# Two-layer attention on one core: scaling q and k after their product, and the second unit's norm moved into blocks 0 and 1

## The chip, the cores and the metric

The kernel runs on one core of a Trainium2 chip. The metric is the device time of one execution in microseconds (us). The engines named below are TensorE (PE, and PEld for its weight loads), VectorE (DVE), ScalarE (ACT), GpSimd (POOL) and SyncE (SP). They run beside each other, each through its own list of instructions in program order, and wait for one another by semaphores.

## What is computed

Sixteen images of 256 channels by 32 x 32 positions go through two layers. Each layer normalises the image over 16 groups, applies a four-headed attention with a position term, and adds the result to the image:

```python
def _L0_conv_ref(x, Wq, bq, Wk, bk, Wv, bv, rel_h, rel_w):
    xf = x.reshape(b, c, n)              # 16, 256, 1024
    def proj(Wt, bt):
        y = jnp.einsum('oc,bcn->bon', Wt, xf) + bt[None, :, None]
        return y.reshape(b, heads, d, n) # 4 heads of 64
    q, k, v = proj(Wq, bq), proj(Wk, bk), proj(Wv, bv)
    sim = jnp.einsum('bhdi,bhdj->bhij', q, k)
    rel = (rel_h + rel_w).reshape(heads, d, n)
    qpos = jnp.einsum('hdi,bhdj->bhij', rel, q)
    attn = jax.nn.softmax(sim + qpos, axis=-1)
    return jnp.einsum('bhdn,bhmn->bhdm', v, attn).reshape(b, c, w, h)

def _gn(v, G=16, eps=1e-5):              # the last axis is split into 16 groups of 2
    g = v.reshape(B_, H_, W_, G, C_ // G)
    m = jnp.mean(g, axis=(1, 2, 4), keepdims=True)
    s = jnp.var(g, axis=(1, 2, 4), keepdims=True)
    return ((g - m) / jnp.sqrt(s + eps)).reshape(v.shape)

x = x + _L0_conv_ref(_gn(x), ...)
x = x + _L1_conv_ref(_gn(x), ...)
```

A group is thus two of the 32 columns of an image, over all channels and rows.

## The kernel before

**Units and blocks.** A unit is one image in one layer; there are 32, in an order (`units`) that lets an image's second layer begin some units after its first. A unit has four blocks, b = 0 to 3: two pairs of heads (`pr`) by two halves of the 1024 positions (`half`). The loop at the end of `fast_path` calls `block(n)` 128 times. A block makes eight tiles of scores (j = 0 to 7): DVE writes the position term into PSUM (`seed`), PE adds the products of k and q onto it (`scores`), ACT takes the exponential to SBUF with a fixed shift in place of the row's maximum. DVE adds up the eight tiles for the denominators, with POOL's accumulating DMAs for the last one. PE multiplies them with v (`attend`), in two stretches of 3.45 us each, and ACT takes the product out of PSUM (`take_out`).

**Stretches.** `stretches` splits a set of products in two halves. The second half waits for a one-element memset on POOL, the token, which in turn waits for the first half; `word()` puts that memset into POOL's list.

**Work for coming units.** Within the blocks stand pieces for later units: `prepare` makes v, q, k and the position products of the next pair or the next unit. The norm of unit u+2 is made in unit u in three steps: `norm_sums` (ACT, one instruction per group with an accumulator that is read out after it, line 190), `norm_mean` (PE multiplies the sums with a constant matrix into the tile pm, line 209, and DVE takes the mean out), `norm_squares` (ACT, line 190 with the bias neg) and `norm_var` (PE line 209 again, DVE, then a power of minus one half and a product on POOL, lines 237 and 239). The scaled image xn of unit u+1 is made in unit u by `norm_apply` (ACT, one instruction per group, line 248). These pieces are cut into ranges of groups and placed by hand at four points of a block: after the first scores, before the second piece, before the first attend stretch, and after the seeds of the next block. In block 1 the third point reads:

```python
if b == 1 and two:
    norm_sums(u + 2, range(12, G))
if b == 1 and one:
    norm_apply(u + 1, range(9, 11))
...
po = psum2(ring[3], f"po_{n}")
values_of_p = attend(blk, po)
values_of_p(0)
if two and half == 1:
    if b == 1:
        mean_out = norm_mean(u + 2, filled(f1, f"pm_{n}", 0.0))
```

On PE the order there is: first attend stretch, the small products of `norm_mean`, the next block's first scores, second attend stretch.

**The beginning.** Unit 0 and unit 1 have nobody to make their norm. So DVE reduces image 0 (`reduced`), PE makes the mean, DVE centres the image (`centred`), ACT squares ten groups and DVE the other six, PE makes the variance and POOL the power (rstd0, line 886). ACT and DVE then scale xn of unit 0 in place (lines 910 and 913), and only then PE multiplies it into q and k. Meanwhile image 1 gets its reductions, mean and squares in the same way. The weights are loaded as they lie and transposed on PE (`transposed`), and ACT copies them out of PSUM (`taken`), in three sets raw0 (first layer's Wq and Wk), raw1 (both Wv) and raw2 (second layer's Wq and Wk).

PSUM has four tiles of two banks with the tags a to d; `ring` says which tag serves which purpose in a block, and changes places within the blocks.

Of the kernel before, what the change touches and what calls it, by code (L numbers as in the profile page):

```python
# [9 lines left out]
F32 = mybir.dt.float32  # L10
# [7 lines left out]
P = 128  # L18
# [34 lines left out]
def fast_path(ctx, tc, sh, x, layers, out, W, den_all, token, good, flag):  # L53
# [140 lines left out]
    def norm_sums(u, gs):  # L194
        if u not in reds:
            reds[u] = small.tile([P, G], F32, tag="red", name=f"red_{u}")
        for g in gs:
            of_group(u, g, AF.Identity, reds[u])
# [27 lines left out]
    def norm_squares(u, gs):  # L226
        for g in gs:
            of_group(u, g, AF.Square, sums[u], bias=negs[u][:, g : g + 1])
# [16 lines left out]
    def norm_apply(u, gs):  # L245
        rstd, shift = rss[u]
        for g in gs:
            nc.scalar.activation(  # L248
                grouped(xns[u], g),
                grouped(xt[units[u][0]], g),  # L250
                AF.Identity,
                bias=shift[:, g : g + 1],
                scale=rstd[:, g : g + 1],
            )
# [333 lines left out]
    ring = ["b", "c", "a", "d"]  # L588
# [29 lines left out]

    def block(n):
# [27 lines left out]
        for j in range(1, 4):  # L647
            scores(blk, j)
        (first, first_out), (second, second_out) = prepare(u, b)
        first(0)  # L650
        if b == 0 and one:
            norm_apply(u + 1, range(0, 1))
        if b == 1 and two:
            norm_sums(u + 2, range(9, 11))
# [3 lines left out]
        if b == 0 and one:  # L658
            norm_apply(u + 1, range(1, 5))
        if b == 1 and two:  # L660
            norm_sums(u + 2, range(11, 12))
        if b == 2 and two:
            norm_squares(u + 2, range(0, 5))
# [19 lines left out]
        add_up(blk, 2)  # L683
        if half == 0:
            second(1)
            second_out()
# [15 lines left out]
        if b == 0 and one:  # L702
            norm_apply(u + 1, range(5, 9))
        if b == 0 and two:
            norm_sums(u + 2, range(0, 2))
        if b == 1 and two:
            norm_sums(u + 2, range(12, G))
        if b == 1 and one:
            norm_apply(u + 1, range(9, 11))
        if b == 2 and two:  # L710
            norm_squares(u + 2, range(5, 11))
        po = psum2(ring[3], f"po_{n}")
        values_of_p = attend(blk, po)
        values_of_p(0)
        if two and half == 1:
            if b == 1:
                mean_out = norm_mean(u + 2, filled(f1, f"pm_{n}", 0.0))
            else:
                mean_out = norm_var(u + 2, filled(f1, f"pm_{n}", EPS / 2))
# [16 lines left out]
        if two and half == 1:  # L736
            mean_out()
# [3 lines left out]
        if b == 0 and two:  # L741
            norm_sums(u + 2, range(2, 9))
        if b == 1 and one:
            norm_apply(u + 1, range(11, G))
        if b == 2 and two:
            norm_squares(u + 2, range(11, G))
# [87 lines left out]
    def by_group(t, g0=0, g1=G):  # L834
        return t.rearrange("p c (w g t) -> p (c w) g t", g=G, t=GT)[:, :, g0:g1, :]

    def spread(t, g0=0, g1=G):
        return (
            t[:, g0:g1].unsqueeze(1).unsqueeze(3).to_broadcast([P, CC * sh.W, g1 - g0, GT])
        )  # L840

    def reduced(u, cc):
        nc.vector.tensor_reduce(
            reds[u][:, cc, :],
            xt[units[u][0]][:, cc, :].rearrange("p (w g t) -> p g w t", g=G, t=GT),
            AX.XY,
            ALU.add,
        )

    def first_mean(u, pm):  # L850
        red = reds.pop(u)
        for cc in range(CC):
            nc.tensor.matmul(pm, W.avg, red[:, cc, :], start=(cc == 0), stop=(cc == CC - 1))
        negs[u] = small.tile([P, G], F32, tag="neg", name=f"neg_{u}")
        nc.scalar.mul(negs[u], pm, -1.0)
        sums[u] = small.tile([P, G], F32, tag="sum", name=f"sum_{u}")
        xns[u] = gnpool.tile([P, CC, N], F32, tag="gn", name=f"xn_{u}")

    def centred(u, g0, g1):
        nc.vector.tensor_tensor(  # L860
            by_group(xns[u], g0, g1),
            by_group(xt[units[u][0]], g0, g1),
            spread(negs[u], g0, g1),
            ALU.add,
        )

    def rest_of_squares(u, g0):

        sq = ppool.tile([P, 2, HALF], F32, tag="p", name=f"first_sq_{u}")
        sq = sq.rearrange("p a n -> p (a n)")[:, : CC * sh.W * (G - g0) * GT].rearrange(  # L870
            "p (w g t) -> p w g t", g=G - g0, t=GT
        )
        nc.vector.tensor_tensor(sq, by_group(xns[u], g0), by_group(xns[u], g0), ALU.mult)
        nc.vector.tensor_reduce(
            sums[u][:, g0:], sq.rearrange("p w g t -> p g w t"), AX.XY, ALU.add
        )

    def first_var(u, pm):
        nc.tensor.matmul(pm, W.avg, sums.pop(u), start=True, stop=True)
        var = small.tile([P, G], F32, tag="var", name=f"var_{u}")  # L880
        nc.vector.tensor_scalar(var, pm, EPS, None, ALU.add)
        return var

    def first_rstd(u, var):
        rstd = small.tile([P, G], F32, tag="rstd", name=f"rstd_{u}")
        nc.gpsimd.tensor_tensor(rstd, var, W.mhalf[:, :G], ALU.pow)
        return rstd

    for u in range(2):
        reds[u] = small.tile([P, CC, G], F32, tag="first_red", name=f"first_red_{u}")  # L890
    G1, G2 = G // 2 + 2, G // 4
    pm0 = psum2("c", "pm_0")
    for cc in range(CC):
        reduced(0, cc)
    first_mean(0, pm0[:, 0, :G])
    transposed("a", *raw0)
    norm_squares(0, range(G1))
    centred(0, 0, G)
    rest_of_squares(0, G1)
    rstd0 = first_rstd(0, first_var(0, pm0[:, 1, :G]))  # L900
    taken(raw0[1])
    transposed("b", *raw1)
    taken(raw1[1])
    pm1 = psum2("d", "pm_1")
    for cc in range(CC):
        reduced(1, cc)
    first_mean(1, pm1[:, 0, :G])
    transposed("a", *raw2)
    for g in range(G2):
        nc.scalar.activation(  # L910
            grouped(xns[0], g), grouped(xns[0], g), AF.Identity, scale=rstd0[:, g : g + 1]
        )
    nc.vector.tensor_tensor(  # L913
        by_group(xns[0], G2), by_group(xns[0], G2), spread(rstd0, G2), ALU.mult
    )
    taken(raw2[1])
    norm_squares(1, range(0, G // 2))
    centred(1, G // 2, G)
    rest_of_squares(1, G // 2)
    (q, q_out), (k, k_out) = (  # L920
        project(0, 0, which, psum2(tag, f"p{which}_0_0")) for which, tag in (("q", "b"), ("k", "c"))
    )
    q(0)
    k(0)
    q(1)
    q_out()
    k(1)
    k_out()
    ab, ab_out = positions(0, 0, psum2("a", "pa_0_0"))
    ab(0)  # L930
    ab_out()
    var1 = first_var(1, pm1[:, 1, :G])
    for j in range(3):
        seed(blocks[0], j, ring[j])
    v, v_out = values(0, 0, psum2("d", "pv_0_0"))
    v(0)
    scores(blocks[0], 0)
# [3 lines left out]
    rstd1 = first_rstd(1, var1)  # L941
    shift1 = small.tile([P, G], F32, tag="nshift", name="nshift_1")
    nc.vector.tensor_tensor(shift1, negs.pop(1), rstd1, ALU.mult)
    rss[1] = (rstd1, shift1)
# [282 lines left out]
```

## Time and profile before

| | |
|---|---|
| median of three runs | 2545.81 us (2545.58 to 2547.84) |
| the profiled execution | 2544.62 us, of which 2542.9 us are the span from the first to the last instruction |
| granted clock of TensorE | 0.998 |
| DVE and ACT busy | 2269.4 us (89%) and 1949.5 us (77%) of the span |
| line 349, seeds on DVE | 1018 instructions of 1228 ns |
| line 394, exponentials on ACT | 1024 instructions of 1114 ns |
| line 190, sums on ACT | 480 of 311 ns |
| line 190, squares on ACT | 498 of 401 ns |
| line 248, applies on ACT | 496 of 495 ns |
| lines 385 and 419 on PE | 8192 and 16384 matmuls |

The profile is of one execution, taken by the hardware. Mean durations are from the start of an instruction to the end of its writing; the next one starts a little before that, so that the distance from start to start is shorter. A list of groups gives, after the sign |, the busy time, the mean duration in ns, and how long the engine had been idle before such instructions and what ended that. Ends of matmuls are modelled. A chain of waits follows the work that ended last back to the start.

### The profile page before, as it was taken

The numbers are of one execution on the slowest core, as the hardware profiler recorded it, in microseconds if no ns is written. First come the engines' busy times: TensorE is split into PE (matmuls) and PEld (weight loads), VectorE is DVE, ScalarE is ACT, GpSimd is POOL, SyncE is SP. The second block draws the span as 40 slices with busy tenths as digits, with TensorE's granted clock in tenths as the row PEclk, the third lists the DMA queues.
The fourth block names the chain that finished last, engine by engine and source line by source line (L and its number), as shares of the span: only waits on it lengthen the run. The fifth ranks groups of instructions, "written<-read, shape, count | busy, mean of one in ns | idle before, by whom it ended". The sixth has DMA issues, their size and how long they took to land.

```text
span 2542.9 us, 86134 instructions
## 1 busy us (share of the span) xinstructions
PE 2514.2 (99%) x37474; PEld 1335.6 (53%) x37474; DVE 2269.4 (89%) x2135; ACT 1949.5 (77%) x3874; POOL 835.1 (33%) x1194
## 2 busy tenths in 40 slices
PE   8999999999999999999999999999999999999997
PEld 4555555555555555555555555555555555555554
DVE  6888998989989889899898898998998998989997
ACT  6778777787777887777877778877778777787753
POOL 1332333323333233333233332333333333323320
PEclk9999999999999999999999999999999999999999
DMA  3344444454444444444444444445445444443441
GB/s 90 70 83 81 77 91 75 78 110 93 87 97 97 87 83 86 95 84 87 100 87 86 88 96 83 83 96 101 82 96 107 81 79 91 75 82 76 86 91 59
DMA packets 119537, 221.05 MB, mean 87 GB/s; under 512 B 53736, under 2 KB 55272, under 8 KB 119152
## 3 DMA queue, kind: packets, MB, share of 16 engines
q0 software_dynamic: 53568, 129.58, 30.7%
q1 hardware_dynamic: 65584, 85.90, 12.2%
q8 instruction: 295, 4.83, 0.8%
q14 instruction: 90, 0.74, 0.1%
HBM read 51.78 MB, written 17.30 MB: 27 GB/s over the span
## 4 chain that ended last, share of the span: by engine, by line
PE 94%; DVE 2%; POOL 1%; issue 1%; DMA 1%; SPq 0%; ACT 0%; POOLq 0%; DVEq 0%; ACTq 0%
PE po L419 33%; PE ps L385 33%; PE pv L298 8%; PE pk L268 8%; PE pq L268 8%; PE pa L326 2%; DVE acc L405 1%; DVE ps L349 1%; POOL rstd L237 1%; DMA stack<-stack 0%; POOL stack L465 0%; POOL stack L460 0%; PE pm L209 0%; DMA x<-in_x_dram 0%; DMA rden<-rd 0%
## 5 line engine op out<-in xcount | busy, mean ns | idle before, releaser
L349 DVE TENSOR_TENSOR ps<-abt 128x1024 f32<-128x1024 f32 x1018 | 1226.8, 1228 | 235.3 <-ACT p L394 147.7
L394 ACT ACTIVATE p<-ps,shift 128x1024 f32<-128x1024 f32 x1024 | 1092.2, 1114 | 323.4 <-PE ps L385 320.5
L385 PE MATMUL ps<-q,k 64*64 64x512 f32 x8192 | 985.5, 590 | 0.8 <-DVE ps L349 0.8
L419 PE MATMUL po<-p,v 64*64 64x256 f32 x16384 | 930.7, 376 | 2.1 <-POOL token L166 2.1
L419 PEld LDWEIGHTS po<-p,v 64*64 64x64 f32 x16384 | 628.9, 133 | 367.2 <-issue 76.9
L405 DVE TENSOR_TENSOR acc<-acc,p 128x1024 f32<-128x1024 f32 x644 | 783.3, 1216 | 7.1
L385 PEld LDWEIGHTS ps<-q,k 64*64 64x64 f32 x8192 | 308.5, 133 | 395.7 <-issue 275.1
L465 POOL DMA_DIRECT2D stack<-stack x310 | 249.6, 805 | 338.7 <-DMA stack<-stack 277.6
L166 POOL MEMSET token<- 1x1 f32 x320 | 35.8, 112 | 830.4 <-PE po L419 400.7
L460 POOL DMA_DIRECT2D stack<-acc x248 | 223.2, 1098 | 71.9 <-DMA stack<-acc 44.1
L298 PE MATMUL pv<-Wv,xn 64*64 64x256 f32 x4096 | 244.4, 376 | 1.6 <-POOL token L166 1.4
L268 PE MATMUL pq<-xn,Wq 64*64 64x512 f32 x2048 | 244.3, 592 | 0.3 <-DVE xn L913 0.3
L268 PE MATMUL pk<-xn,Wk 64*64 64x512 f32 x2048 | 242.8, 589 | 0.0
L248 ACT ACTIVATE xn<-x,nshift,rstd 128x128 f32<-128x128 f32 x496 | 209.9, 495 | 18.2 <-POOL nshift L239 18.2
L298 PEld LDWEIGHTS pv<-Wv,xn 64*64 64x64 f32 x4096 | 153.3, 133 | 104.3 <-issue 48.3
L190 ACT ACTIVATE junk<-x,neg 128x128 f32<-128x128 f32 x498 | 195.1, 401 | 0.0
L436 POOL DMA_DIRECT2D acc<-p x124 | 115.5, 931 | 227.8 <-ACT od L480 128.5
L441 POOL DMA_DIRECT2D acc<-acc x124 | 109.5, 883 | 206.0 <-DMA acc<-p 197.0
L480 ACT COPY od<-po 128x512 f32<-128x512 f32 x127 | 74.4, 586 | 118.9 <-PE po L419 118.9
L403 DVE TENSOR_TENSOR acc<-p,p 128x1024 f32<-128x1024 f32 x128 | 156.3, 1221 | 0.0
L268 PEld LDWEIGHTS pq<-xn,Wq 64*64 64x64 f32 x2048 | 78.6, 134 | 142.1 <-issue 136.7
L190 ACT ACTIVATE junk<-x 128x128 f32<-128x128 f32 x480 | 144.8, 311 | 0.0
(74 smaller groups left out, 1118.8 us busy)
## 6 DMA issues: line engine op xcount, KB each, us to landing
acc<-p POOLq DMA_DIRECT2D x124, 512.0 KB, 5.1
rden<-rd SPq DMA_DIRECT2D x126, 256.0 KB, 4.1
acc<-acc POOLq DMA_DIRECT2D x124, 256.0 KB, 3.6
x<-in_x_dram SPq DMA_DIRECT2D x32, 512.0 KB, 5.1
stack<-acc SPq DMA_DIRECT2D x248, 64.0 KB, 2.1
stack<-acc POOLq DMA_DIRECT2D x248, 64.0 KB, 3.3
out_dram<-x SPq DMA_DIRECT2D x31, 512.0 KB, 5.1
stack<-stack POOLq DMA_DIRECT2D x62, 128.0 KB, 2.9
```

The costliest lines, as they stand in the source:

```text
L190: nc.scalar.activation(junk, grouped(xt[units[u][0]], g), func, accum_out=into[:, g : g + 1], **bias)
L248: nc.scalar.activation(grouped(xns[u], g), grouped(xt[units[u][0]], g), AF.Identity, bias=shift[:, g : g + 1], scale=rstd[:, g : g + 1],)
L268: yield nc.tensor.matmul(pk[c, nh, :], w[l][rs, cc, c0 : c0 + D], xns[u][rs, cc, nh * HALF : (nh + 1) * HALF], start=(t == 0 and cc == 0), ...
L298: yield nc.tensor.matmul(pv[c, a, i, :], xns[u][rs, cc, j0 : j0 + D], W.wv[l][rs, cc, :], start=(t == 0 and cc == 0 and i == 0), stop=(t = ...
L349: nc.vector.tensor_tensor(ps.rearrange("p h (w y) -> p h w y", y=H), ab[:, :, :H].unsqueeze(2).to_broadcast([P, 2, XH, H]), ab[:, :, H + h ...
L385: nc.tensor.matmul(ps[c, h, :], a[hs, j0 : j0 + D], b[hs, columns], start=bool(tag) and i == 0, stop=i == len(terms) - 1, skip_group_check ...
L394: nc.scalar.activation(p, ps, AF.Exp, bias=W.shift)
L403: nc.vector.tensor_tensor(accs[blk], probs[blk, 0], probs[blk, 1], ALU.add)
L405: nc.vector.tensor_tensor(accs[blk], accs[blk], probs[blk, j], ALU.add)
L419: yield nc.tensor.matmul(po[c, a, :QUART], vts[u][rs, j, c0 : c0 + D], p[rs, h, a * QUART : (a + 1) * QUART], start=(t == 0 and j == 0), s ...
L460: nc.gpsimd.dma_start(at, acc[R:D, h, :], accum_op=ALU.add)
L465: nc.gpsimd.dma_start(stack[:rows_], stack[rows_ : 2 * rows_], accum_op=ALU.add)
```

## The change

First, q and k of unit 0's first pair are multiplied from the centred image, before the variance is known; DVE multiplies them by rstd on the way out of PSUM (`scaled`, four instructions of 512 columns) and ACT adds the biases. DVE scales the centred image as well, for v and the later products, in two halves (`first_scaled`). The variance product of unit 0 stands behind the first q stretch on PE, and raw1's transposes ahead of it; raw2's come after the first position products.

Second, unit 1 keeps only its reductions and mean in the beginning, with three groups of squares. The other thirteen, its variance and all of its `norm_apply` stand in blocks 0 and 1. The sums of unit 2, which ACT made in those blocks, become two reductions on DVE.

Third, the ranges of all blocks are now in tables, and a helper `norms(u, b, i)` issues what stands at point i of a block: applies first, then sums, then squares. The ring starts with other tags, and scores 1 of the first block is issued ahead of it.

```diff
     def norm_apply(u, gs):
-        rstd, shift = rss[u]
         for g in gs:
+            rstd, shift = rss[u]
...
-    ring = ["b", "c", "a", "d"]
+    ring = ["c", "a", "b", "d"]
...
+    APPLY = {0: (0, 1, 5, 9, 9), 1: (9, 9, 9, 11, G)}
+    SUMS = {0: (0, 0, 0, 2, 9), 1: (9, 11, 12, G, G)}
+    SQUARES = {2: (0, 0, 5, 11, G)}
+
+    FIRST_SQUARES = {0: (3, 5, 9, G, G)}
+    FIRST_APPLY = {1: (0, 1, 4, 8, G)}
+
+    def norms(u, b, i):
+        def groups(table):
+            return range(*table.get(b, (0,) * 5)[i : i + 2])
+
+        if u + 1 < NU:
+            norm_apply(u + 1, groups(APPLY if u > 0 else FIRST_APPLY))
+        if u == 0:
+            norm_squares(1, groups(FIRST_SQUARES))
+        elif u + 2 < NU:
+            norm_sums(u + 2, groups(SUMS))
+        if u + 2 < NU:
+            norm_squares(u + 2, groups(SQUARES))
...
-        for j in range(1, 4):
+        for j in range(1 if n > 0 else 2, 4):
             scores(blk, j)
...
-        if b == 0 and one:
-            norm_apply(u + 1, range(0, 1))
-        if b == 1 and two:
-            norm_sums(u + 2, range(9, 11))
+        norms(u, b, 0)
+        if n == 1:
+            reduced(2, 1)
+            added(2)
...
         add_up(blk, 2)
+        if n == 0:
+            reduced(2, 0)
...
-        if b == 0 and one:
-            norm_apply(u + 1, range(5, 9))
-        if b == 0 and two:
-            norm_sums(u + 2, range(0, 2))
-        if b == 1 and two:
-            norm_sums(u + 2, range(12, G))
-        if b == 1 and one:
-            norm_apply(u + 1, range(9, 11))
-        if b == 2 and two:
-            norm_squares(u + 2, range(5, 11))
+        norms(u, b, 2)
         po = psum2(ring[3], f"po_{n}")
         values_of_p = attend(blk, po)
         values_of_p(0)
+        if n == 0:
+            mean_out = norm_var(1, filled(f1, f"pm_{n}", EPS / 2))
...
-        if two and half == 1:
+        if two and half == 1 or n == 0:
             mean_out()
...
+    def scaled(into, t, rstd):
+
+        shape = dict(g=G, t=GT)
+        nc.vector.tensor_tensor(
+            into.rearrange("p (w g t) -> p w g t", **shape),
+            t.rearrange("p (w g t) -> p w g t", **shape),
+            spread(rstd, XH),
+            ALU.mult,
         )
...
+    pm0 = psum2("d", "pm_0")
     for cc in range(CC):
         reduced(0, cc)
-    first_mean(0, pm0[:, 0, :G])
+    first_mean(pm0[:, 0, :G])
     transposed("a", *raw0)
-    norm_squares(0, range(G1))
-    centred(0, 0, G)
-    rest_of_squares(0, G1)
-    rstd0 = first_rstd(0, first_var(0, pm0[:, 1, :G]))
+    transposed("b", *raw1)
+    norm_squares(0, range(4))
     taken(raw0[1])
...
+    norm_squares(0, range(4, G // 2 + 1))
+    nc.vector.tensor_tensor(
+        by_group(xns[0]), by_group(xt[0]), spread(negs[0], CC * sh.W), ALU.add
+    )
+    rest_of_squares(G // 2 + 1)
+    pq, pk = psum2("c", "pq_0_0"), psum2("a", "pk_0_0")
+    q, k = project(0, 0, "q", pq)[0], project(0, 0, "k", pk)[0]
+    q(0)
+    q.word()
+    nc.tensor.matmul(pm0[:, 1, :G], W.avg, sums.pop(0), start=True, stop=True)
+    var = small.tile([P, G], F32, tag="var", name="var_0")
+    nc.vector.tensor_scalar(var, pm0[:, 1, :G], EPS, None, ALU.add)
+    rstd = small.tile([P, G], F32, tag="rstd", name="rstd_0")
+    nc.gpsimd.tensor_tensor(rstd, var, W.mhalf[:, :G], ALU.pow)
+    taken(raw1[1])
     for cc in range(CC):
         reduced(1, cc)
...
+    added(1)
+    pm1 = filled("d", "pm_1", 0.0)
     k(0)
     q(1)
-    q_out()
     k(1)
-    k_out()
-    ab, ab_out = positions(0, 0, psum2("a", "pa_0_0"))
+    kqs = {}
+    for which, bias, ps in (("q", W.bq, pq), ("k", W.bk, pk)):
+        t = kqs[which] = kqpool.tile([P, N], F32, tag=which, name=f"{which}_0_0")
+        for nh in range(NH):
+            scaled(t[:, nh * HALF : (nh + 1) * HALF], ps[:, nh, :], rstd)
...
+    biased("q", W.bq, 0)
+    biased("q", W.bq, 1)
+    biased("k", W.bk, 0)
+    qs[0, 0], ks[0, 0] = kqs["q"], kqs["k"]
+    mean_out = norm_mean(1, pm1)
+    ab, ab_out = positions(0, 0, psum2("b", "pa_0_0"))
     ab(0)
     ab_out()
+    biased("k", W.bk, 1)
+    mean_out()
...
+    first_scaled(0)
+    transposed("d", *raw2)
+    taken(raw2[1])
+    seed(blocks[0], 0, ring[0])
+    scores(blocks[0], 0)
+    seed(blocks[0], 1, ring[1])
+    seed(blocks[0], 2, ring[2])
     v, v_out = values(0, 0, psum2("d", "pv_0_0"))
     v(0)
-    scores(blocks[0], 0)
+    norm_squares(1, range(3))
+    first_scaled(1)
+    scores(blocks[0], 1)
     v(1)
     v_out()
```

## The prediction

> **What bounds the kernel now.** First the page's busy times and its chain that ended last:
>
> ```profile
> PE 2514.2 (99%) x37474; PEld 1335.6 (53%) x37474; DVE 2269.4 (89%) x2135; ACT 1949.5 (77%) x3874; POOL 835.1 (33%) x1194
> PE 94%; DVE 2%; POOL 1%; issue 1%; DMA 1%; SPq 0%; ACT 0%; POOLq 0%; DVEq 0%; ACTq 0%
> ```
>
> TensorE sets the end. Matmul ends are modelled, so I check this by stretch. The view by windows, cut at the first matmul of line 209 in successive units:
>
> ```profile
> 0.00:30.00 30.00, 19.67 (x196) 12.55 (x196) 16.12 (x19) 16.21 (x52) 3.81 (x9) 1.00 0.50 162
> 224.03:301.86 77.83, 77.83 (x1172) 41.24 (x1168) 70.20 (x67) 61.30 (x125) 26.27 (x38) 1.00 0.42 76
> 2251.56:2329.39 77.83, 77.83 (x1172) 41.23 (x1168) 70.68 (x68) 61.48 (x125) 26.91 (x38) 1.00 0.42 77
> ```
>
> Columns after the stretch: length, then busy time of PE, PEld, DVE, ACT, POOL. A unit takes 77.83 us early and late, all of it PE; so a microsecond that PE waits in the middle is a microsecond on the end. Only the first 30 us hold a third of idle PE. The chain of waits there, in order of time:
>
> ```profile
> 13.20 2.94 POOL rstd L886
> ...
> 16.17 1.77 DVE xn L913
> ...
> 18.07 3.48 PE pq L268 x16
> 21.55 1.72 PE pk L268 x16
> ...
> 28.00 0.19 DVE var L881
> ...
> 28.23 1.96 PE pv L298 x32
> 30.19 1.01 PE ps L385 x8
> ```
>
> The first q stretch waits for the scaled xn, hence for rstd; from 18.07 on PE hardly waits. The last view is the timeline of block 1 of unit 1, where all the trouble I expect lies:
>
> ```profile
> 142.29 1.12 ACT L394 ACTIVATE p<-ps,shift 128x1024 f32<-128x1024 f32 x1
> 143.29 0.33 ACT L190 ACTIVATE junk<-x 128x128 f32<-128x128 f32 x1
> ...
> 144.17 0.33 ACT L190 ACTIVATE junk<-x 128x128 f32<-128x128 f32 x1
> 144.38 0.21 ACT L190 ACTIVATION_READ_ACCUMULATOR junk<-x 128x1 f32 x1
> 144.47 0.89 ACT L248 ACTIVATE xn<-x,nshift,rstd 128x128 f32<-128x128 f32 x2
> 144.85 0.37 PEld L209 LDWEIGHTS pm<-red,avg 64*64 64x64 f32 x8
> 145.06 0.25 PE L209 MATMUL pm<-red,avg 64*64 64x16 f32 x8
> ```
>
> The reader is to see that the last of the four sums ends at 144.38 + 0.21 = 144.59, the two applies come after it, and PE reaches the matmuls that read these sums (red) at 145.06: a slack of 0.47 us. I read the same place in unit 14 (sum ends 1160.05 + 0.21, matmul 1160.74: 0.48) and unit 29 (2328.72 + 0.19, 2329.39: 0.48). It is the same in every unit, since ACT and PE repeat one pattern.
>
> [...] the first stretch takes 3.48 us, the next, of equal work, 1.72. [...] pm's weights load at 144.85, ahead of their matmuls. [...] For the new DVE scaling, [...] The trace has 1.22 us at 1024 and 2.29 at 2048[...].
>
> **The change, part by part.** (a) *Every unit from 1 on, block 1, point 2* (before the first attend stretch). Before: sums 12 to 15 of unit u+2, then applies 9 and 10 of unit u+1. The new helper always calls the applies first. Nothing is added or dropped; ACT does the same work by 145.37. But the sums end two applies later: the first apply starts at 144.47 and the second at 144.87 (line 248's instructions one by one), so 0.395 each, 2 x 0.395 = 0.79. They end at 144.59 + 0.79 = 145.38. From the end of a releaser to the matmul it frees this trace shows about 0.05 (DVE's var ends 28.19 by the chain, pv starts 28.23), so pm starts at 145.43 instead of 145.06, 0.37 later; a stretch restarted from a wait loses some more (the po stretch at 147.12, begun from a POOL wait, has its second group of four after 0.267 us where 0.216 is usual, so 0.05). I take 0.40 per unit, 0.36 to 0.50. Behind pm on PE stand the next block's first scores (line 385), then the second attend stretch: all of PE moves. The loss is not made good, as PE has no other slack in the unit. Units 1 to 29 have both u+1 and u+2 and b = 1: 29 x 0.40 = 11.6 us. In two of them (units 1 and 5) the attend stretch right behind already waits for a POOL token that a DMA chain holds up (2.1 us in two waits by the list of waits, the longer 1.2); there the new wait falls into the old one: minus 2 x 0.4 = 0.8. Net of (a): +10.8.
>
> (b) *The beginning.* q and k come from the centred values (DVE until 7.91 + 2.30 = 10.21), and no longer wait for rstd; their rstd is applied by four DVE operations from PSUM. On PE stand ahead of them both sets of transposes, the second needing raw1, which lands about 7.2 us after its issue at 3.6 to 4.1, so at 11.3; eight transposes take 1.95, of which half can go before: q(0) starts at 12.4, cold, 3.45, to 15.85. The variance matmul is queued behind it (0.6), then var 0.19 and pow 2.93 (the other instance took 3.55): rstd at 19.6 instead of 16.14, later, but with k(0) and q(1) beside it (2 x 1.72, to 19.7). The token of k's second stretch is a POOL memset behind the pow, so k(1) runs 19.75 to 21.5. DVE: x_1's two reductions (2.34) fit under q and k; scalings at 0.65 spacing: q 19.8 to 21.1, k 21.6 to 22.9. ACT adds the biases (0.56 each by line 137's copy of that size), q until 21.7; pa 21.75 to 22.7; ACT's copy of abt to 23.9. DVE: the mean of unit 1 0.18, xn's first half scaled (2 x 0.63) to 24.25, first seed 1.2: first scores at 25.5. The third transposes (1.95, from 23.05) and their copies (to 26.1) lie under that. What followed at 28.23 (v, scores 0, v, scores 1 to 3, until 35.50) takes 6.9 without gaps, until 32.4: a lead of 3.1. Its bounds are 2.0 and 4.2: [...] the pow may take 3.55.
>
> (c) *Blocks 0 and 1 of unit 0.* Squares 9 to 15 of unit 1 (7 x 0.39 on ACT, the spacing of line 190 with neg) stand between exp 7 and the variance matmul. ACT was free at 47.17 with the attend stretch over at 49.27; squares end at 47.17 + 2.8 = 50.0, PE waits about 0.85 (0.4 to 1.2), with the next block's scores 0 behind it. In block 1 three applies (1.2) instead of one sum (0.3) stand ahead of ACT's copy of abt, which the seed of scores 7 needs: at most 0.35. DVE's reductions of x_2 (1.17 each) fall in idle spells of 1.8 and 1.95 us ahead of seeds; unit 1's pow is on POOL beside attend. On SP nothing moves. Lead left: 3.1 - 0.85 - 0.35 = 1.9.
>
> (d) Ring order, tile names and the tables elsewhere: 0, the same tiles rotate and all other points keep their order.
>
> Sum: +10.8 - 1.9 = +8.9 on the profiled execution (2542.9 span and 1.7 around it, 2544.62): 2553.5. The median of the three runs is 1.2 above that execution: 2545.8 + 8.9 = 2554.7.
>
> **The rivals.** *Only the beginning counts*: PE doesn't feel the swap, since slack of 0.47 is all but enough. For: only the pm matmul needs red, and its weights load early. Against: 0.79 + 0.05 is above 0.47 by 0.37 and the pattern repeats to 0.01 us. It holds only if a pair of applies takes under 0.42 us. Result 2545.8 - 1.9 = 2543.9, down to 2542; not slower than before. *The wait costs more*: PE restarts at pm with weights unloaded, each group of four paying one load of 0.13 in the open, 0.55 a unit: 29 x 0.55 = 16, less 1 and 1.9: 2559. Against: the restarts in the trace lose only 0.05. *The beginning is late too*: the variance matmul behind a cold q(0), a token behind a pow, the DVE scaling in front of the seeds; lead 0 after the stalls of (c), or worse: 2556.6 to 2558. *The POOL chain absorbs more*: other token waits (four at block 3's pv, 1.4 in all by the list of waits, behind the pow) shrink. But these hang on var, which PE's own pm releases, so they move along; at most 2 us: 2552.7.
>
> **How the numbers follow.** Forecast with its bounds (2550.5 to 2557): 0.74, of which 0.02 falls below 0.2%, about 5 us, which a measurement of this kernel can just tell from no change; the costlier wait 0.07; late beginning 0.06; POOL absorbs 0.05, of which 0.02 below; swap not felt 0.08, of which 0.03 faster by over 0.2%. Low end: 29 x 0.36 - 2 - 3.7 = +4.7; high end: 29 x 0.5 - 0.8 - 0.5 = +13.2: 2550.5 to 2559. Slower 0.88, same 0.09, faster 0.03.
>
> **What would show it.** Right: in block 1 of every unit from 1 on, line 248's two applies stand ahead of line 190's four sums, pm waits for ACT, and the period from pm to pm is 78.2 instead of 77.83; the waits list shows PE pm behind ACT with about 29 waits of 0.4. First scores near 25.5, and one PE wait of 0.85 at block 0's pm. Wrong: a period of 77.83, or first scores after 30.

## The result and the profile after

The changed kernel takes 2558.53 us (median of six, 2557.84 to 2560.41) against 2546.43 us for the kernel before beside it (six, 2543.05 to 2547.84): a ratio of 1.0051 with a 95% interval of 1.0041 to 1.0062, slower by 12.1 us. Against the median shown earlier, 2545.81, it is 12.7. The forecast was +8.9 us, 2554.7, with bounds of 2550.5 to 2557 for its main case and up to 2559 with all rivals. The measured time is above the bounds of the main case and just inside the wider ones. The profiled execution took 2558.64 us, of which 2556.9 are span, 14.0 more than the span before.

The page's busy times and the shares of the chain that ended last, after:

```profile
PE 2520.7 (99%) x37484; PEld 1329.6 (52%) x37484; DVE 2271.3 (89%) x2145; ACT 1946.3 (76%) x3853; POOL 836.7 (33%) x1195
PE 86%; ACT 5%; issue 3%; DMA 2%; POOL 2%; DVE 1%; SPq 0%; ACTq 0%; POOLq 0%; DVEq 0%
```

PE still sets the end and its busy time hardly shows the loss: 6.5 of the 14.0 us. In the chain PE went from 94% to 86%, and ACT from 0% to 5%: PE now waits regularly for something of ACT. The view by windows says where. Two units, again cut at successive first matmuls of line 209, and the first 30 us (length, then busy time of PE, PEld, DVE, ACT and POOL, the clock, the DMA share and GB/s):

```profile
0.00:30.00 30.00, 20.26 (x234) 11.58 (x238) 19.41 (x27) 14.60 (x39) 3.85 (x10) 1.00 0.51 163
222.48:300.73 78.25, 78.07 (x1172) 40.94 (x1168) 70.20 (x67) 61.38 (x125) 26.94 (x38) 1.00 0.41 76
2264.52:2342.77 78.25, 78.06 (x1172) 41.14 (x1168) 70.61 (x68) 61.36 (x125) 26.55 (x38) 1.00 0.41 76
```

A unit takes 78.25 us in place of 77.83, with the same 1172 matmuls and nearly the same work on ACT, early and late alike. So it isn't work that was added; it is one wait per unit. The timeline of block 1 of unit 1, after:

```profile
141.09 1.12 ACT L394 ACTIVATE p<-ps,shift 128x1024 f32<-128x1024 f32 x1
142.09 0.91 ACT L248 ACTIVATE xn<-x,nshift,rstd 128x128 f32<-128x128 f32 x2
142.87 0.33 ACT L190 ACTIVATE junk<-x 128x128 f32<-128x128 f32 x1
...
143.77 0.32 ACT L190 ACTIVATE junk<-x 128x128 f32<-128x128 f32 x1
143.97 0.21 ACT L190 ACTIVATION_READ_ACCUMULATOR junk<-x 128x1 f32 x1
...
144.24 0.30 PE L209 MATMUL pm<-red,avg 64*64 64x16 f32 x8 [0.19 <-ACT junk L190]
...
144.37 1.07 PE L385 MATMUL ps<-q,k 64*64 64x512 f32 x8
```

The applies of line 248 now stand ahead of the four sums, the last sum is read out at 143.97 + 0.21 = 144.18, and pm starts at 144.24, on that release. Before, the same sums were done 0.47 us ahead of pm. PE's waits by engine and line (us in total, times, longest), after:

```profile
PE pm L209 <- ACT junk L190: 6.2, 30, 0.8
PE pv L298 <- POOL token L166: 4.8, 4, 2.6
...
PE po L419 <- POOL token L166: 2.0, 2, 1.2
```

and of the kernel before, the two lines to be set beside them:

```profile
PE po L419 <- POOL token L166: 2.1, 2, 1.2
...
PE pv L298 <- POOL token L166: 1.4, 4, 0.3
```

The first line after is new: 30 waits, one per unit from 1 on and one, the longest, in block 0. The list counts only time in which PE had nothing in flight by its modelled ends (0.19 of each). Measured from start to start, as the distance beyond the usual one of 0.196, the 29 waits are 10.6 us, 0.365 each. The pv line grew by 3.4 us, where the forecast had no growth; the po line stayed.

Measured from start to start, the 14.0 us come to: the beginning (to line 209's product of the sums of squares in unit 0's block 3) 106.15 to 104.95, -1.2; the 29 units 2262.16 to 2277.37, +15.2, of which 29 x (0.365 + about 0.04 of restart) = 11.8 are the pm wait, and +3.2 the waits for POOL's token (4.6 to 7.8); what follows the units 174.55 to 174.56. Some 0.2 are unassigned.

### The profile page after: what moved, and what is told of

Read it like the earlier page. It is cut to its first block, busy times and chain, and to the rows that moved or that the text cites. A ratio compares the mean times of both kernels' runs of the same rounds, so it can differ in the third digit from the quotient of the medians.

```text
span 2556.9 us, 86147 instructions
## 1 busy us (share of the span) xinstructions
PE 2520.7 (99%) x37484; PEld 1329.6 (52%) x37484; DVE 2271.3 (89%) x2145; ACT 1946.3 (76%) x3853; POOL 836.7 (33%) x1195
## 3 DMA queue, kind: packets, MB, share of 16 engines
q1 hardware_dynamic: 65584, 85.90, 12.1%
## 4 chain that ended last, share of the span: by engine, by line
PE 86%; ACT 5%; issue 3%; DMA 2%; POOL 2%; DVE 1%; SPq 0%; ACTq 0%; POOLq 0%; DVEq 0%
PE ps L385 30%; PE po L419 29%; PE pk L268 8%; PE pv L298 8%; PE pq L268 8%; ACT p L394 3%; PE pa L326 2%; ACT junk L190 1%; ACT xn L248 1%; POOL rstd L237 1%; DMA stack<-stack 1%; PE pm L209 0%; DVE acc L405 0%; DMA acc<-p 0%; DVE ps L349 0%
## 5 line engine op out<-in xcount | busy, mean ns | idle before, releaser
L441 POOL DMA_DIRECT2D acc<-acc x124 | 114.7, 925 | 186.3 <-DMA acc<-p 176.9
```

## The experiments

The tables give the median of a kernel's runs and its ratio to the kernel before in the same runs. Where the text speaks of token waits, they are from start to start: `po` before the second attend stretch, `pv` before the second v stretch.

### One part alone: the swap, and all but the swap

Theory: ACT's order in block 1 costs 0.4 us in every unit and the rest of the change gives 1 to 2 us. Rival: the new beginning costs time as well.

The swap put alone into the kernel before (`before_swap`):

```diff
+        if b == 1 and one:
+            norm_apply(u + 1, range(9, 11))
         if b == 1 and two:
             norm_sums(u + 2, range(12, G))
-        if b == 1 and one:
-            norm_apply(u + 1, range(9, 11))
```

> The kernel before with one thing changed: in block 1, point 2 of each of 30 units (unit 0 too), applies 9 and 10 are issued ahead of sums 12 to 15. My theory: the order alone costs 0.42 us a unit at the pm matmul (0.37 of wait and 0.05 of restart, as the changed kernel's profile shows), 30 x 0.42 = 12.6 us, and POOL's token waits at pv may move the sum by 3 either way: 2558 to 2562, the list of PE's waits has pm behind ACT 30 times with 6.2 us. Rival: the order costs little by itself, and what the changed kernel lost came from its new beginning (another phase of POOL's DMA chain against PE): under +6 us, or pm waits without a longer period.

The whole change, but with the old order at this one point (`after_unswap`):

```diff
+        sums_first = u > 0 and b == 1 and i == 2
+        if sums_first and u + 2 < NU:
+            norm_sums(u + 2, groups(SUMS))
         if u + 1 < NU:
             norm_apply(u + 1, groups(APPLY if u > 0 else FIRST_APPLY))
...
-        elif u + 2 < NU:
+        elif u + 2 < NU and not sums_first:
             norm_sums(u + 2, groups(SUMS))
```

> The changed kernel with the old order (sums 12 to 15 ahead of applies 9 and 10) in block 1, point 2 of units 1 to 29, all else as changed. My theory: 29 waits at pm go and what is left is the new beginning with its lead of 1.2 us: 1 to 2 us under the kernel before, and 13 to 14 under the changed kernel; POOL's waits at pv fall back from 4.8 to about 1.4. Rival: the beginning itself shifts POOL's DMA chain, the pv waits of 4.8 stay: about 2 us above the kernel before.

And the dose: only one apply ahead of the sums (`before_one_ahead`: apply 9, sums, apply 10), or three (`before_three_ahead`: applies 9 to 11, sums, and applies 12 on at the point after the seeds).

> The kernel before with only apply 9 ahead of the four sums, apply 10 behind them. My theory is a threshold: one apply delays the sums by 0.39, the slack is 0.48 with about 0.05 of it for the way from ACT to PE, so pm is just in time: no wait at pm, time within 1.5 us of the kernel before. Rival, a cost for each apply that stands ahead: half of the swap's, +6 us.

> The kernel before with applies 9, 10 and 11 ahead of the four sums (11 is taken from point 3). My theory: the wait grows by one apply, 0.37 + 0.39 = 0.76, and 0.05 of restart: 30 x 0.81 = 24 us, so about +24 (22 to 28). Rival, a fixed cost of a broken matmul stream: as with two ahead, +12.6; a cost for each apply: 1.5 times that of two, +19.

| kernel | us | ratio (95%) | against 2546.14 | a unit at its shortest |
|---|---|---|---|---|
| one apply ahead | 2545.92 | 0.9998 (0.9989 to 1.0006) | -0.2 | 77.85 |
| two ahead, `before_swap` | 2557.04 | 1.0041 (1.0027 to 1.0055) | +10.9 | 78.24 |
| three ahead | 2568.72 | 1.0084 (1.0071 to 1.0098) | +22.6 | 78.62 |
| changed kernel, old order, `after_unswap` | 2551.23 | 1.0017 (1.0010 to 1.0023) | +5.1 | 77.83 |

The waits of the kernel with three applies ahead, with the same columns as above:

```profile
PE pm L209 <- ACT junk L190: 17.3, 30, 0.6
```

and one of its units in the view by windows:

```profile
224.50:303.12 78.62, 78.06 (x1172) 41.15 (x1168) 70.25 (x67) 61.29 (x125) 26.44 (x38) 1.00 0.41 76
```

The first apply is free, since 0.395 fits into the slack of 0.47; each further one adds 0.38 to 0.40 to the unit, and the list has no line for PE's pm of line 209 with one ahead. So the slack and its price are shown. The swap by itself costs 10.9 us by the medians, where the forecast had 10.8 for this part. That they agree so closely is partly chance: the interval reaches from 6.9 to 14.0, the expectation for this run was 12.6, and its profiled span is 12.3 above that of the kernel before, which is 30 x 0.41.

The last row of the table was a miss. With the swap taken back the changed kernel should have been a little faster than the kernel before; it was 5.1 us slower. Its unit is 77.83, its pm waits are gone but for the one in block 0, and its beginning is shorter (103.96 against 106.15). What it has is waits for POOL. PE's waits, changed kernel with the old order:

```profile
PE pv L298 <- POOL token L166: 5.4, 6, 2.6
PE po L419 <- POOL token L166: 3.1, 1, 3.1
```

From start to start the two make 9.8 us against 4.6 before. So a second cause stood beside the swap, and the two don't add: +10.9 and +5.1 alone, +12.1 together.

### Why POOL's token is late

The token of pv's second stretch in block 3 stands in POOL's list behind the power of line 237. The place where it costs most is unit 23. The timeline there, before:

```profile
1898.54 0.77 POOL L465 DMA_DIRECT2D stack<-stack  x1 [1.96 <-DMA stack<-stack]
1901.07 0.09 POOL L166 MEMSET token<- 1x1 f32 x1 [1.75 <-PE pm L209]
1901.51 0.80 POOL L465 DMA_DIRECT2D stack<-stack  x1 [0.36 <-issue]
1905.05 1.69 POOL L460 DMA_DIRECT2D stack<-acc  x2 [2.74 <-issue]
1906.67 4.19 POOL L237 TENSOR_TENSOR rstd<-var,mhalf 128x16 f32<-128x16 f32 x1
...
1912.56 1.96 PE L298 MATMUL pv<-Wv,xn 64*64 64x256 f32 x32 [0.35 <-POOL token L166]
```

and after:

```profile
1909.16 0.77 POOL L465 DMA_DIRECT2D stack<-stack  x1 [2.02 <-DMA stack<-stack]
1910.34 0.09 POOL L166 MEMSET token<- 1x1 f32 x1 [0.41 <-PE pm L209]
1912.41 0.80 POOL L465 DMA_DIRECT2D stack<-stack  x1 [1.98 <-DMA stack<-stack]
1915.95 1.69 POOL L460 DMA_DIRECT2D stack<-acc  x2 [2.74 <-issue]
1917.57 4.87 POOL L237 TENSOR_TENSOR rstd<-var,mhalf 128x16 f32<-128x16 f32 x1
...
1924.07 1.96 PE L298 MATMUL pv<-Wv,xn 64*64 64x256 f32 x32 [2.58 <-POOL token L166]
```

Line 465 folds the rows of denominators by DMAs, each of which POOL issues once the one before has landed. The token behind the pm products is a mark of PE's own time. Before, the next fold starts 0.44 us after that token; now it starts 2.07 after it, since POOL first waits 1.98 for a fold to land. The delay begins with the first fold of the block. POOL issues it 8.59 us ahead of line 209's second product in both kernels, and it lands 3.10 us later before and 4.39 after; all folds behind it move back. Then comes a gap of 2.74 us that is the same in both (more on it at the end), a power of 4.87 us in place of 4.19, and PE waits 2.58 us.

Is the power the link? It was replaced by a product of the same shape in three kernels (the scaling of the images is thereby another; all instructions but this one stay). The product takes POOL 0.5 to 1.7 us:

```diff
-        nc.gpsimd.tensor_tensor(rstd, var, W.mhalf[:, :G], ALU.pow)
+        nc.gpsimd.tensor_tensor(rstd, var, W.mhalf[:, :G], ALU.mult)
```

> The kernel before, with the power on POOL that every norm from unit 2 on makes (line 237) replaced by a product of the same shape, so rstd is a wrong number and the output another; it takes POOL's 3.9 us away and leaves all else. My theory now: the tokens at pv that PE waits for (1.4 to 2.1 us a run[...]) are late because the pow stands ahead of them on POOL; without it those waits are gone: 2 to 4 us under the kernel before. Rival: the tokens are late because of the DMA chain alone; no change.

> The changed kernel in the old order of sums and applies, with the same product in place of the pow (another output). My theory: its 5 us over the kernel before are POOL tokens that come later against PE, as the new beginning puts PE at another phase to POOL's chain; with the pow gone both kernels lose these waits and the beginning shows its own worth: 1 to 1.5 us UNDER the same edit of the kernel before. Rival: the loss sits elsewhere (blocks 0 and 1, the tail), then it stays 4 to 5 us above that kernel.

> The changed kernel with the product in place of the pow (another output). My theory: 29 waits of 0.42 at pm stay and nothing else, 12.2 above the old order with the same edit and so about 11 above the kernel before with the same edit. Rival, that the swap and the tokens work on each other by more than the pow: under 10 or over 13.

| kernel, with a product for the power | us | ratio (95%) | against 2546.34 | gain by it |
|---|---|---|---|---|
| before | 2542.10 | 0.9981 (0.9974 to 0.9988) | -4.2 | 4.2 |
| changed, old order | 2544.51 | 0.9989 (0.9982 to 0.9995) | -1.8 | 6.9 |
| changed | 2552.90 | 1.0024 (1.0016 to 1.0031) | +6.6 | 5.5 |

The gains are against each kernel's own distance above. The waits of the kernel before with the product, of which no pv line is left:

```profile
PE po L419 <- POOL token L166: 1.8, 1, 1.8
```

In the two others 0.3 us of pv waits remain in one wait each. So the power is a link in the pv waits. It isn't in the po wait of unit 5, which stays in all three (1.8, 2.7 and 1.0 us).

The expectation for the kernel before was about right; the two others were misses. Without the power the new beginning was to lead by 1 to 1.5 us, and it still loses 2.4 to the old one (-1.8 against -4.2): about half of the 5.1 went with the power. And the swap was to cost 12.2 and costs 8.4, the outcome of the rival. In the profiles most of both differences is one po wait, that of unit 5: the unit with it is longer than the shortest by 4.5 us with the old order, 1.8 more than that wait itself, by 2.0 in the kernel before, and by 1.3 with the swap. Why it differs so was not tried.

### Getting the variance earlier

If the token is late because of what stands ahead of it on POOL, an earlier variance might help. `spread_early` takes the old order, spreads unit 1's squares and applies otherwise over blocks 0 and 1, and lets DVE take the variance out of PSUM earlier in block 3, right after `fold_stack`, so that POOL's power comes earlier too:

```diff
-    FIRST_SQUARES = {0: (3, 5, 9, G, G)}
-    FIRST_APPLY = {1: (0, 1, 4, 8, G)}
+    FIRST_SQUARES = {0: (3, 6, 11, G, G)}
+    FIRST_APPLY = {1: (0, 2, 3, 8, G)}
...
+        early = two and b == 3
+        if early:
+            mean_out()
...
-        if two and half == 1 or n == 0:
+        if two and half == 1 and not early or n == 0:
             mean_out()
```

> A version meant to beat both: the changed kernel with sums ahead of applies again, unit 1's squares spread over block 0 as 3, 5 and 5 and its first applies as 2, 1, 5 and 8 (so that the waits of 0.97 at block 0's pm and 0.38 at block 1's seed 7 go), and in block 3 the variance's pow right behind the first fold instead of behind the last (the output is the same). My theory: 1.3 from block 0 and 1, and most of the waits at pv: 2 to 4 us under the kernel before, 2542 to 2544. Rival: the pow now holds up the folds behind it, whose later DMAs are waited for at po: nothing gained over the kernel before, or slower.

2582.10 us, 1.0138 (1.0123 to 1.0154), +35.8: a miss. DVE's timeline in block 3 of a late unit:

```profile
2402.80 0.19 DVE L235 TENSOR_REDUCE var<-pm 128x16 f32<-128x32 f32 x1 [1.45 <-PE pm L209]
2402.90 1.21 DVE L530 TENSOR_TENSOR od<-od,rden 128x1024 f32<-128x1024 f32 x1
2404.15 1.28 DVE L537 SCALAR_TENSOR_TENSOR x<-od,bv,x 128x1024 f32<-128x1024 f32 x1
2405.36 2.36 DVE L349 TENSOR_TENSOR ps<-abt 128x1024 f32<-128x1024 f32 x2
```

and PE's waits in the same kernel:

```profile
PE ps L385 <- DVE ps L349: 22.9, 31, 1.2
```

Reading the variance earlier in DVE's list doesn't produce it earlier; DVE waits 1.45 us for PE, `finish` (lines 530 and 537) and the seeds queue behind it, and PE then waits for the seeds in every unit. It is the same kind of error as the swap, on another engine. The token waits did fall, from 8.5 us in the list of the changed kernel with the old order to 3.8 here, so the folds behind the power are not what costs. The finer spreading itself did as wished in the beginning: no wait at block 0's pm, and a beginning of 103.24 us.

### Nothing but PE instructions: the phase of the instruction packets

What else differs in unit 23, long after the beginning? Not the order on any engine. But what ran in the beginning has other counts, and the one followed here is PE's: 37484 matmul records against 37474. Instructions are themselves brought in by DMA, which the page lists as queues. The largest, before and after alike:

```profile
q8 instruction: 295, 4.83, 0.8%
```

These are 295 packets of 16 KB, one in about 8 us (median). PE has 2 x 37474 records of matmuls and weight loads, 254 for each packet, so I take them for PE's instructions, about 256 in a packet; a kernel below with 256 records more has 296 packets. The page gives the queue's time as a share of the core's 16 DMA engines, as it does for the queue of the folds. By this estimate ten matmuls, with a weight load for each, are 20 of 256 instructions, and move every later packet against PE's work by 20/256 of 8 us, 0.6 us. In the trace the packet nearest to line 209's second product, in the 30 units with a norm, stands about 0.5 us (median) earlier against it than before. That this does harm was only a guess, so it was tried: a few small products into an unused tile of PSUM, ahead of the first mean, where PE is idle (its first matmul starts at 5.72 us), are added to the kernel before. Their result goes nowhere.

```diff
+    pad = psum2("d", "pad")
+    for i in range(5):
+        nc.tensor.matmul(
+            pad[QUARTERS[i % 2], 0, :G], W.avg[LO, :D], W.avg[LO, :G],
+            start=True, stop=True, skip_group_check=True,
+        )
     pm0 = psum2("c", "pm_0")
```

Five of them make ten records (each product in float32 appears as two), as many as the change adds; 64 make 128, with their weight loads 256 records, and the page then counts 296 packets. In the changed kernel 59 make the ten up to one packet: in the kernel with the old order (`unswap_pad59`), in that with the finer spreading as well but without the early variance (`spread_pad59`), and in the changed kernel (`after_pad59`).

> The kernel before with five tiny matmuls added at PE's start, where it is idle until 5.7 us: about 20 PE instructions more ahead of all others, no time of their own. [...] the changed kernel has 19 PE records more ahead of unit 1 than the kernel before, so its packets fall 0.7 to 1.4 us earlier within each unit, and in unit 23 it then has one fold's landing 1.4 us later. My theory: that phase is what makes POOL's tokens late. Five matmuls give the kernel before the phase of the changed one: +3 to +6 us, pv and po waits near 7 to 10 instead of 4. Rival, the phase is nothing and the new beginning's loss has another cause: within 1 us of the kernel before.

> The control: 64 tiny matmuls, 256 PE instructions, a whole packet, in the same idle time of PE. My theory: same phase as the kernel before, so the same time within 1 us. Rival, what counts is any added work at the start: as before_pad5 or more.

> The changed kernel with the old order of sums and applies and 59 tiny matmuls at PE's start (236 instructions and the 19 records it has more make 255, about a whole packet): the phase of the kernel before. My theory: POOL's waits fall back to about 4 and the beginning's lead of 1.3 us shows: 1 to 2 us under the kernel before, 5 to 6 under the same without the matmuls. Rival: it stays at 2551.

> A version meant to beat both: as unswap_pad59, and unit 1's squares spread over block 0 as 3, 5 and 5 and its first applies as 2, 1, 5 and 8, which took the waits of 0.97 at block 0's pm and 0.38 at block 1's scores away in another run. My theory: 1.3 us more off, 2.5 to 3.5 under the kernel before. Rival: as unswap_pad59 or worse.

> The changed kernel itself with the 59 tiny matmuls at PE's start. My theory: the swap's 29 x 0.405 = 11.75 stay, the lead of 1.3 less the 0.5 to 1 that the matmuls take from it, and POOL's waits fall from 7.8 in the changed kernel's profile to 4 to 6: 10.5 to 12 us over the kernel before, 0.5 to 2.5 under the changed kernel. Rival: the phase acts only with the old order, where PE reaches the tokens 0.4 us earlier; then it stays at 12 to 13 over the kernel before.

| kernel | packets moved by (us) | us | ratio (95%) | against before of these runs |
|---|---|---|---|---|
| before, 5 products | -0.5 | 2552.34 | 1.0015 (1.0007 to 1.0023) | +4.8 |
| before, 64 products | 0.0 | 2548.78 | 1.0006 (0.9997 to 1.0014) | +1.2 |
| changed, old order (from above) | -0.4 | 2551.23 | 1.0017 (1.0010 to 1.0023) | +5.1 |
| the same, 59 products | 0.1 | 2547.36 | 0.9997 (0.9989 to 1.0006) | -0.2 |
| finer spreading, old order, 59 products | 0.1 | 2546.88 | 0.9998 (0.9989 to 1.0006) | -0.7 |
| changed (from above) | -0.5 | 2558.53 | 1.0051 (1.0041 to 1.0062) | +12.1 |
| the same, 59 products | 0.1 | 2556.48 | 1.0045 (1.0032 to 1.0057) | +11.9 |

Five products that nobody reads cost 4.8 us; 64 cost 1.2, with an interval that holds none (-0.8 to 3.6). The intervals of the two overlap; their medians, of 13 runs each side by side, are 3.6 us apart. Filling up to a whole packet takes the 5.1 us of the new beginning away. The products aren't quite free: in the profiles, which scatter by a microsecond there, they make the beginning 0.3 us longer with 5, 0.9 with 64, and 0.9 to 2.2 with 59. So most of the 1.2 of the 64 is their own time, and the two kernels that were to beat the one before, by 1 to 2 and by 2.5 to 3.5 us, came out level with it. PE's waits in the kernel before with five products:

```profile
PE pv L298 <- POOL token L166: 4.8, 4, 2.6
PE po L419 <- POOL token L166: 3.2, 1, 3.2
```

They are close to those of the changed kernel with the old order (5.4 and 3.1). The other counts that differ between the changed kernel and the one before, such as ACT's or DVE's, stay as they are when products are added. So in these two kernels the place of the packets moves the time, both ways, with nothing else changed but the short added work at the start.

The traces show how a fold near a packet fares. In unit 23 the first fold of block 3, the one above that landed after 3.10 and 4.39 us, is issued at the same point of PE's work in all fifteen profiled executions. Where a packet starts 1.5 to 2.4 us after it (seven of them: 1.56 in the changed kernel, 2.36 in the kernel before with five products), it lands after 4.4 to 4.7 us. Where the packet starts after 2.45 to 2.65 us (eight: 2.64 in the kernel before), it lands after 2.8 to 3.1 in six and 4.6 to 4.7 in two. It is not this fold alone: the fifth fold of a unit, in the kernel before, takes 2.15 us (median) in the 21 units without a packet start near it (from 0.9 us ahead of its issue to 1.9 behind) and 3.31 in the 10 with one. Why a fold with a packet near it lands later is not shown.

Three reservations. The packets' place changes how often the long waits come, not whether they can: with packets in the old place, the kernel with one apply ahead has a pv wait of 2.6 us in unit 9, and that with 64 products has two of 1.5. Single executions scatter accordingly, those of the kernel before from 2543.5 to 2551.0 in one set, and the profile of the old order with 59 products still has 8.7 us of token waits, in an execution whose span alone, 2550.1, is above the median of its runs; so the medians carry the verdict. And in the changed kernel itself the gain is not shown by the medians: it is 2.0 us lower with 59 products, but the kernel before was 1.9 lower in that set of runs too (2544.54), so against it 12.1 became 11.9, and the two ratios overlap. Its profile has 4.8 us of token waits in place of 7.8, and a beginning 0.9 longer.

No kernel of the study that computes the same beats the one before beyond the interval; its order at this point should be kept.

## Why the prediction was right and where it failed

**Right: the mechanism of the swap and its size.** The swap pushes the four sums 0.79 us back past a slack of 0.47, and PE stops at pm with all its later work behind it. That all of PE moves with pm was assumed; the unit of 78.25 us in place of 77.83, with the same 1172 matmuls, shows it. Forecast 0.40 per unit, 11.6 in all; measured 0.40 to 0.42 by the period, 11.8. The swap alone, in 30 units, as there unit 0 has it too, did +10.9. In its profile one of the two waits ahead of attend stretches did vanish (2.4 to 1.4 us of po token waits), as the 0.8 of part (a) had it, but the pv waits grew by 0.6, so the token waits together fell by 0.4 only. The rival that PE doesn't feel the swap is out, and so is the restart with open weight loads (0.55 a unit).

**Right, with small errors: the beginning.** The chain of waits of the changed kernel, from the landing of raw1 on:

```profile
3.67 7.50 DMA raw<-in_L_conv_Wv_dram
...
13.19 2.94 PE pq L268 x16
16.13 0.32 PE pm L911 x2
16.45 1.88 PE pk L268 x16
18.33 1.72 PE pq L268 x16
20.05 1.71 PE pk L268 x16
...
22.44 0.68 DVE k L849
...
24.41 1.16 DVE ps L349
25.57 0.04 issue
25.61 1.09 PE ps L385 x8
```

First scores at 25.61, forecast 25.5 (before, the first v started at 28.23 and the first scores at 30.19). That it fits so well is in part luck: q(0) started 0.8 us later than assumed, as all of raw1's transposes came first, but its stretch took 2.94 us, 0.5 less than the 3.45 of the forecast (the first stretch before took 3.48). The DVE scaling of 512 columns takes 0.68 us; a line through the two durations read before, 1.22 at 1024 and 2.29 at 2048, gives 0.69 as an estimate. Block 0's pm waits 0.97 from start to start (0.79 in the list), forecast 0.85; block 1's copy of abt costs 0.38, forecast at most 0.35. Of a lead of 1.9 us, 1.2 is left in this profile, and 2.2 in that of the same beginning with the old order; four profiles of this beginning reach from 103.96 to 105.34, so these are single readings.

**Wrong: that the rest is nothing.** The step that failed is the sum over what comes after the beginning: part (d) set everything else at 0, and (a) took 0.8 off at POOL's tokens. In the changed kernel the token waits grew by 3.2 us instead, and with the swap taken back by 5.2. The wait of 1.1 us in unit 1 that (a) counted on did go; unit 5's stayed (1.35 to 1.40), and unit 7 got a new one of 0.93. The four pv waits of about 0.52 each (units 6, 9, 16 and 23) became 0.53, 1.69, 0.53 and 2.75 (units 1, 9, 16 and 23). A rival spoke of POOL's chain, but only to say that it would absorb more: the sign was wrong. The reason given against absorption, that these tokens hang on var and so move along with PE, holds only where var is the last to come; in unit 23 a fold's landing comes later. The list of waits for the forecast had these waits, 1.4 us in four, so the tokens were already late there, and a shift of POOL's chain against PE could show. That should have been priced from both sides, by about 3 us each way. What shifted the chain is the place of PE's instruction packets, after 20 more instructions on PE, as far as the runs with added products show it: clearly in the kernel before and in the old order, in the changed kernel itself only by the profiles. No view read for the forecast showed it.

By the number alone, two rivals lie nearer to 2558.53 than the forecast: the costlier wait (2559) and the late beginning (2556.6 to 2558). Both are wrong: the unit lost 0.40 to 0.42 and not 0.55, and the beginning was earlier.

**The sum.** -1.2 (forecast -1.9), +11.8 (11.6), +3.2 (-0.8): 13.8 of the 14.0 us of the two profiled executions, and +12.1 by the medians. Of the 4.9 between 13.8 and the forecast 8.9, the token waits are 4.0. That the swap and the phase together cost less than their sum (10.9 + 5.1) fits with PE, 0.4 us later at each pm, waiting less for a token behind it; in unit 23 both wait 2.6 us, and behind that the changed kernel runs at a granted clock of 1.00, that with the old order at 0.50 to 0.54, as told below. This split was read from profiles, not tried by itself.

## What to carry to other kernels

Work of two kinds on one engine, of which only one has a consumer soon, has an order that matters: read the slack between the producer's last instruction and its consumer in the trace (here 0.47 us) and compare it with what is put ahead of it (here 0.395 for each instruction); the first fitted and the second cost 0.4 us in every unit. A helper that issues pieces in one fixed sequence at all points changes that order silently. When token or DMA waits already stand in the list with a few tenths each, put a range of some microseconds of both signs on every change of this size, even one that adds only a handful of instructions far away.

## What the runs showed of the hardware

**The place of the instruction packets moved the time in two kernels.** Five useless products moved the time by 4.8 us of 2547, and 59 that filled up to a whole packet moved it back in another kernel. A fold with a packet beside it landed later, in one place of the unit after 3.31 in place of 2.15 us (medians).

**PE at half rate after short waits.** The view by windows, changed kernel with the old order, the stretch of pv behind its 2.58 us token wait in unit 23, and a stretch ahead of it:

```profile
1910.50:1912.00 1.50, 1.50 (x20) 0.45 (x12) 1.50 (x3) 0.00 (x0) 1.50 (x1) 1.00 0.03 3
1914.96:1917.00 2.04, 2.04 (x20) 1.28 (x24) 1.23 (x1) 1.75 (x5) 0.09 (x1) 0.54 0.87 162
1917.00:1918.40 1.40, 1.40 (x20) 0.89 (x16) 0.00 (x0) 0.00 (x0) 0.00 (x0) 0.50 1.14 129
```

The same stretch in the changed kernel, behind a wait of the same length:

```profile
1924.07:1925.80 1.73, 1.73 (x32) 1.27 (x36) 1.23 (x1) 1.73 (x5) 0.09 (x1) 1.00 0.54 84
```

The third column from the end is the granted clock: 0.50 to 0.54 in the one, 1.00 in the other. The 32 matmuls of the stretch take 3.60 us in the one and 1.96 in the other. So after a wait of 2.58 us the clock was lower once and not the other time; what decides it is not shown. In all kept traces together, 9 of 13 token waits of 1.87 to 3.23 us were followed by a stretch at about half clock, and none of the 23 of 0.9 to 1.8. Such a wait thus cost 1.5 to 2 us beyond itself, or nothing.

**Gaps on POOL that wait for nothing shown.** Six times in a run POOL stands for 2.3 to 6.5 us ahead of a DMA, with no releaser, as the 2.74 us above. They come at the same POOL instructions in all fifteen traces, each 121 of POOL's DMAs after the last. Three of the waits that vary most, in units 5, 9 and 23, stand 3.5 to 7.5 us behind the end of such a gap in the kernel before. The cause of the gaps was not tried.

**The power on POOL is long and uneven:** for 128 x 16 elements 3.2 to 4.9 us in the units; the product in its place took 0.5 to 1.7.
